# Self-attention with the scale inside the exponential and the division after the values' product

## The chip, the cores and the metric

The kernel runs on one core of one Trainium2 chip. The core has a matrix engine (TensorE, PE in the profile), a vector engine (VectorE, DVE), an activation engine (ScalarE, ACT), GpSimd (POOL) and a queue engine (SyncE, SP), each with its own in-order stream of instructions; they wait for one another by semaphores. The metric is the device time of one execution in microseconds. The time before is 3067.56 us, the median of three runs (3067.09 to 3067.82).

## The reference

Four layers act on 128 tokens of 256 features. Each layer has a cross attention over a context of 12544 tokens, a self-attention among the 128 tokens, and a feed-forward part with experts; each adds to the residual. The change touches the self-attention of layers 1, 2 and 3 (layer 0 has another kind). Cut to what matters:

```
layer 1:  a1 = softmax(q1 k1 / 4);  a2 = softmax(q2 k2 / 4)     # 16 heads, each split in two halves of 8
          out = (a1 - lam * a2) @ v;  out = out / rms(out) * norm_w * 0.2
layer 2:  out = softmax(rope(q) rope(k) / 4) @ v                # 16 heads of 16
layer 3:  out = softmax(where(causal, q k / 8, -inf)) @ v       # 16 heads of 64
```

Layer 1 has thus 32 score matrices of 128 x 128, layers 2 and 3 have 16 each.

## The kernel before, in words

A class `Net` writes the whole program as one trace of tile operations. A scheduler then puts the instructions of each engine in an order: except in stretches that the kernel holds in order by hand (`in_order`, in the cross attentions), an engine's order need not be that of the source. Tiles come from pools with a fixed number of buffers, and an instruction that needs a buffer waits until the last reader of its former content is done.

`run` (L1730) goes through the layers: cross attention, self-attention, feed-forward. While layer 1's self-attention runs, the first eight key and value blocks of layer 2's cross attention are made as well (`keys_biased`, L977, called from L1758): PE projects the context (L102) into the one PSUM pair `kv`, ACT empties it into keys (L132) and values (L136), and only then can the next block use the pair. Their context tiles `ctxA` and `ctxB` are loaded through GpSimd's queue (L393, L395). In layer 2 the weights of the experts and the few tokens `lastA`, `lastB` for layer 3 are loaded during the self-attention, through SP's queue.

The self-attention's core is a generator, `weights_among` (L1291). For each group it spreads the keys over heads with a mask (`keys`, L1298, on DVE), and then makes tiles of four score matrices, 128 queries by 4 x 128 keys, in one PSUM bank `ps` (L278 through `mm`); there are three such banks in this stage. Each tile goes through these steps:

- DVE scales the scores out of PSUM into `e` (L296 through `ts`), or in layer 3 scales and adds the causal mask in one operation (L292 through `stt`);
- `softmax` (L469): maximum (L473), subtraction (L289 through `tt`), both on DVE; exponential on ACT (L475); sum (L477), reciprocal (L478) and division, a product with the broadcast reciprocal (L289), on DVE.

`values_among` (L1315) turns the weights by PE (`tr`, L1320), copies them to SBUF as `eT` (in turn DVE L284 and ACT L286), multiplies with the values into `acc` (L278) and copies the result to `o` (L1326, DVE). Layer 1 first combines the two halves of each head, `a = e0 + lam * e1` (L1368, L292 through `stt`), so that its tile of four matrices gives two heads. There are eight tiles in layer 1, four in layer 2 and four in layer 3. Tiles `e` have three buffers, `tr` two banks, `acc` one.

After its loop layer 1 normalises `o` (L1371 to L1381, with a square root on ACT, L1377), copies it to `turned`, multiplies by `wo` (L278) and adds the residual. The normalisation of the next part makes `xn` (L298), which PE turns (`tr`, L450) for the router.

Of the kernel before, what the change touches and what calls it, by code (L numbers as in the profile page):

```python
# [16 lines left out]
AF = mybir.ActivationFunctionType  # L17
ALU = mybir.AluOpType
AX = mybir.AxisListType
PSUM = bass.MemoryType.PSUM  # L20

P = 128
# [22 lines left out]
def bc(ap, axis, n):  # L45

    ap = ap.unsqueeze(axis)
    shape = list(ap.shape)
    shape[axis] = n
    return ap.to_broadcast(shape)  # L50
# [155 lines left out]
class Net:  # L206
# [1083 lines left out]

    def weights_among(self, pool, qT, kT, ng, hpg, mask, scale, causal=None):  # L1291

        nc = self.nc
        per = max(1, 4 // hpg)
        for g in range(0, ng, per):
            keys = pool.tile([P, per, hpg, P], F32, tag="keys", name="keys")
            for i in range(per):
                self.tt(keys[:, i], bc(kT[:, g + i, :], 1, hpg), bc(mask, 2, P), ALU.mult)  # L1298
            for a in range(0, per * hpg, 4):
                p = self.ps()  # L1300
                if per > 1:
                    for i in range(per):
                        self.mm(p[:, i * hpg * P : (i + 1) * hpg * P], [(qT[:, g + i, :], keys[:, i].rearrange("p h t -> p (h t)"))])
                else:
                    self.mm(p, [(qT[:, g, :], keys[:, 0, a : a + 4, :].rearrange("p h t -> p (h t)"))])
                p = p.rearrange("p (h t) -> p h t", h=4)
                e = pool.tile([P, 4, P], F32, tag="e", name="e", bufs=3)
                if causal is None:
                    self.ts(e, p, scale, None, ALU.mult)
                else:  # L1310
                    self.stt(e, p, scale, bc(causal, 1, 4), ALU.mult, ALU.add)
                self.softmax(e, e, (4, P))
                yield g * hpg + a, e

    def values_among(self, pool, out, h, e, n, v, hd):  # L1315

        nc = self.nc
        t = self.tr()
        for i in range(n):
            nc.tensor.transpose(t[:, i, :], e[:, i, :], self.ident)  # L1320
        eT = pool.tile([P, 4, P], F32, tag="eT", name="eT")
        self.evac(eT[:, :n], t[:, :n])
        p = self.acc()
        for i in range(n):
            self.mm(p[:, i * hd : (i + 1) * hd], [(eT[:, i, :], v[:, (h + i) * hd : (h + i + 1) * hd])])
        nc.vector.tensor_copy(out[:, h * hd : (h + n) * hd], p[:, : n * hd])  # L1326

    def dot_exp(self, pool, a, b):
        d = self.d
# [8 lines left out]
    def l1_attn(self, x):  # L1338
        nc, d = self.nc, self.d
        with self.tc.tile_pool(name="a1", bufs=2, reuse_waits="tile") as pool:  # L1340
            wqkv = self.load_w(d["L1_attn_w_qkv"], 2, 3 * D, "wqkv")
            wo = self.load_w(d["L1_attn_wo"], 2, D, "wo")
            norm = self.all_rows(d["L1_attn_norm_w"], D, "norm", pool)
            m8 = self.group_mask(16, 8, 1.0, "m8g")
            l1, l2 = self.dot_exp(pool, "q1", "k1"), self.dot_exp(pool, "q2", "k2")
            lam = pool.tile([P, 1], F32, tag="lam", name="lam", bufs=1)
            self.tt(lam, l2, l1, ALU.subtract)
            self.ts(lam, lam, LAMBDA_INIT, None, ALU.subtract)

            xT = self.normed(x)  # L1350
            qT = pool.tile([P, 2, P], F32, tag="qT", name="qT", bufs=1)
            kT = pool.tile([P, 2, P], F32, tag="kT", name="kT", bufs=1)
            for i, t in ((0, qT), (2, kT)):
                for g in range(2):
                    p = self.ps()
                    c = slice((i + g) * P, (i + g + 1) * P)
                    self.mm(p[:, :P], [(wqkv[:, k, c], xT[:, k, :]) for k in range(2)])
                    self.evac(t[:, g, :], p[:, :P])
            v = pool.tile([P, D], F32, tag="v", name="v", bufs=1)
            p = self.ps()  # L1360
            self.mm(p[:, :D], [(xT[:, k, :], wqkv[:, k, 2 * D :]) for k in range(2)])
            self.evac(v, p[:, :D])

            o = pool.tile([P, D], F32, tag="o1", name="o1", bufs=1)
            for h, e in self.weights_among(pool, qT, kT, 2, 16, m8, 0.25):
                pairs = e.rearrange("p (h two) t -> p h two t", two=2)
                a = pool.tile([P, 2, P], F32, tag="a", name="a")
                self.stt(a, pairs[:, :, 1, :], lam, pairs[:, :, 0, :], ALU.mult, ALU.add)  # L1368
                self.values_among(pool, o, h // 2, a, 2, v, 16)

            heads = lambda t: t.rearrange("p (h e) -> p h e", h=H)  # L1371
            t = pool.tile([P, D], F32, tag="sq", name="sq")
            self.tt(t, o, o, ALU.mult)
            r = self.stat()
            nc.vector.tensor_reduce(r, heads(t), AX.X, ALU.add)
            self.ts(r, r, 1.0 / 16, 1e-6, ALU.mult, ALU.add)
            nc.scalar.activation(r, r, AF.Sqrt)  # L1377
            nc.vector.reciprocal(r, r)
            self.ts(r, r, 1.0 - LAMBDA_INIT, None, ALU.mult)
            self.tt(heads(o), heads(o), bc(r, 2, 16), ALU.mult)  # L1380
            self.tt(o, o, norm, ALU.mult)  # L1381

            turned = pool.tile([P, 2, 16, 8], F32, tag="turned", name="turned", bufs=1)
            for c in range(2):
                nc.vector.tensor_copy(turned[:, c], o.rearrange("p (g c e) -> p c e g", c=2, e=16)[:, c])
            p = self.ps()
            self.mm(p[:, :D], [(turned[:, c].rearrange("p e g -> p (e g)"), wo[:, c, :]) for c in range(2)])
            return self.residual(x, p[:, :D])

    def l2_attn(self, x):  # L1390
        nc, d = self.nc, self.d
        with self.tc.tile_pool(name="a2", bufs=2, reuse_waits="tile") as pool:
            w = [self.load_w(d[f"L2_attn_{k}T"], 2, D, k) for k in ("wq", "wk", "wv", "wo")]
            turns = pool.tile([P, 2, 8], F32, tag="turns", name="turns", bufs=1)
            nc.sync.dma_start(turns, d["rope"])
            cos, sin = turns[:, 0, :], turns[:, 1, :]
            xT = self.normed(x)
            qkv = pool.tile([P, 3, D], F32, tag="qkv", name="qkv", bufs=1)
            for i in range(3):
                p = self.ps()  # L1400
                self.mm(p[:, :D], [(xT[:, k, :], w[i][:, k, :]) for k in range(2)])
                self.evac(qkv[:, i, :], p[:, :D])
            qk = qkv[:, :2, :].rearrange("p i (h e two) -> p (i h) e two", e=8, two=2)
            roped = pool.tile([P, 2 * H, 8, 2], F32, tag="roped", name="roped", bufs=1)
            re, im = qk[:, :, :, 0], qk[:, :, :, 1]
            c, s = bc(cos, 1, 2 * H), bc(sin, 1, 2 * H)
            t = pool.tile([P, 2 * H, 8], F32, tag="t", name="t", bufs=1)
            self.tt(roped[:, :, :, 0], re, c, ALU.mult)
            self.tt(t, im, s, ALU.mult)
            self.tt(roped[:, :, :, 0], roped[:, :, :, 0], t, ALU.subtract)  # L1410
            self.tt(roped[:, :, :, 1], re, s, ALU.mult)
            self.tt(t, im, c, ALU.mult)
            self.tt(roped[:, :, :, 1], roped[:, :, :, 1], t, ALU.add)
            qkT = self.transposed(roped.rearrange("p h e two -> p (h e two)"), 4, pool, "qkT")
            o = self.ap.tile([P, D], F32, tag="o", name="o")
            for h, e in self.weights_among(pool, qkT[:, :2], qkT[:, 2:], 2, 8, self.m16, 0.25):
                self.values_among(pool, o, h, e, 4, qkv[:, 2, :], 16)
            return self.project_out(x, o, w[3])

    def l3_attn(self, x):  # L1420
        nc, d = self.nc, self.d
        dims = H * 64
        with self.tc.tile_pool(name="a3", bufs=2, reuse_waits="tile") as pool:
            causal = pool.tile([P, P], F32, tag="causal", name="causal", bufs=1)
            nc.gpsimd.memset(causal, 0.0)
            nc.gpsimd.affine_select(
                out=causal, in_=causal, pattern=[[-1, P]], compare_op=ALU.is_ge, fill=NEG, base=0, channel_multiplier=1
# [18 lines left out]
                self.evac(v[:, n : n + 512], p)  # L1446
            wo = self.load_w(d["L3_attn_w_o"], 8, D, "w_o")
            o = pool.tile([P, dims], F32, tag="o3", name="o3", bufs=1)
            for h, e in self.weights_among(pool, *qkT, 8, 2, self.m64, 0.125, causal):
                self.values_among(pool, o, h, e, 4, v, 64)  # L1450
            return self.project_out(x, o, wo, pool=pool, n=8)


# [368 lines left out]
```

## Time and profile before

| what | time |
|---|---|
| median of three runs | 3067.56 us |
| the profiled execution | 3067.74 us |
| its span, first to last instruction | 3066.0 us |
| PE busy | 2916.9 us (95%) |
| DVE busy | 2233.8 us (73%) |
| ACT busy | 1436.4 us (47%) |
| POOL busy | 457.6 us (15%) |
| mean granted TensorE clock | 0.969 |
| loop of layer 1's self-attention | 1211.5 to 1251.9 us of the span |
| loop of layer 2's | 1848.3 to 1872.95 us |
| loop of layer 3's | 2955.3 to 2982.5 us |

The span is that of one execution under the hardware profiler, 1.74 us shorter than the device time of that execution. Busy times are sums over the whole span; a matmul of 32-bit floats shows as two records. The granted clock is what the chip let TensorE run at in a stretch, as a share of full speed. In the rows below, `out<-in` names the tile an instruction writes and those that it reads, and "idle before, releaser" says how long its engine had stood and what it then waited for. Line numbers are those of the kernel before.

### The profile page before, as it was taken

To read this page: it belongs to the slowest core of one execution; us is meant where nothing else is said; L and a number is where in the kernel's file an instruction comes from. 1 tells how busy PE (TensorE), PEld (TensorE's weight loads), DVE (VectorE), ACT (ScalarE), POOL (GpSimd) and SP (SyncE) were. 2 spreads that over 40 slices of the span, in tenths; PEclk is the share of its full clock that TensorE was granted. 3 is DMA by queue.
4 is the path that set the end of the run, shared out by engine and by line. 5 is a ranking of instruction groups with operands and counts; after the bars stand their busy time and mean duration, and the time that the engine had idled before them with its cause. 6 is when DMAs were issued, how large, how long until landed. Compare 5 with 4: busy or idle time off the path is not lost.

```text
span 3066.0 us, 78435 instructions
## 1 busy us (share of the span) xinstructions
PE 2916.9 (95%) x34893; PEld 2205.6 (72%) x34893; DVE 2233.8 (73%) x2864; ACT 1436.4 (47%) x1694; POOL 457.6 (15%) x502
## 2 busy tenths in 40 slices
PE   8999999989999998899999997999999999999979
PEld 5677667455676576765776664689989889889858
DVE  6876877549997897779668754367777777777844
ACT  1176148321582285211852571355556556556521
POOL 6676676212000000110000000100000000000000
PEclk9999999999999999899999996999999999999979
DMA  4201210561002202421012015432222222222436
GB/s 128 61 19 32 68 40 4 192 218 56 21 3 73 63 5 91 150 78 42 18 37 70 24 30 180 145 97 85 86 78 87 84 81 86 80 85 84 122 112 208
DMA packets 166857, 246.95 MB, mean 81 GB/s; under 512 B 21261, under 2 KB 108431, under 8 KB 166520
## 3 DMA queue, kind: packets, MB, share of 16 engines
q1 hardware_dynamic: 160200, 227.67, 24.2%
q0 software_dynamic: 6208, 14.27, 1.6%
q8 instruction: 274, 4.49, 0.6%
q14 instruction: 63, 0.52, 0.1%
q10 hardware_dynamic: 112, 0.01, 0.0%
HBM read 241.75 MB, written 0.13 MB: 79 GB/s over the span
## 4 chain that ended last, share of the span: by engine, by line
PE 81%; DVE 11%; issue 3%; ACT 2%; POOL 2%; DMA 2%; SPq 0%; DVEq 0%; POOLq 0%; ACTq 0%
PE pair L102 19%; PE pair L551 9%; PE v L102 8%; PE acc L658 8%; PE sc L796 6%; PE acc L838 6%; PE pair L592 4%; PE ps L278 4%; PE one L592 4%; DVE parts L552 4%; PE kv L102 2%; DVE e L292 2%; PE acc L278 2%; PE pair L585 2%; PE ps L1609 1%
## 5 line engine op out<-in xcount | busy, mean ns | idle before, releaser
L552 DVE TENSOR_REDUCE parts<-pair 128x2 f32<-128x1024 f32 x600 | 679.1, 1197 | 103.6 <-PE pair L551 101.8
L102 PE MATMUL pair<-ctxA,wk 128*128 128x256 f32 x1236 | 329.0, 399 | 1.4 <-ACT kT L193 1.1
L102 PEld LDWEIGHTS pair<-ctxA,wk 128*128 128x128 f32 x1236 | 217.2, 190 | 140.6 <-DVE parts L552 95.2
L551 PE MATMUL pair<-kT,qz 32*128 32x512 f32 (+1 forms) x1632 | 270.1, 608 | 6.9 <-DVE parts L552 6.8
L289 DVE TENSOR_TENSOR top<-top,kept 128x1024 f32<-128x1024 f32 (+2 forms) x145 | 169.1, 1169 | 134.4 <-ACT kept L798 133.2
L798 ACT COPY kept<-sc 128x1024 f32<-128x1024 f32 (+1 forms) x135 | 136.3, 1010 | 252.0 <-PE sc L796 252.0
L292 DVE SCALAR_TENSOR_TENSOR e<-pair,floor 128x1024 f32<-128x1024 f32 x196 | 230.4, 1219 | 9.1 <-PE pair L592 3.0
L612 ACT ACTIVATE e<-e 128x1024 f32<-128x1024 f32 x196 | 207.2, 1057 | 45.5 <-DVE e L292 38.1
L636 ACT ACTIVATE e<-pair 128x1024 f32<-128x1024 f32 x196 | 200.6, 1024 | 53.0 <-PE pair L592 32.2
L592 PE MATMUL pair<-qz,kT 32*128 32x256 f32 x2112 | 219.1, 374 | 0.0
L658 PE MATMUL acc<-e,v 128*17 128x128 f32 x6336 | 211.4, 274 | 3.1 <-ACT e L651 2.2
L536 POOL TENSOR_SCALAR row<-mask 128x512 bf16<-128x512 uint8 (+1 forms) x100 | 189.8, 1898 | 151.3 <-PE pair L551 96.7
L132 ACT ACTIVATE kT<-pair,bk 128x512 f32<-128x512 f32 (+1 forms) x68 | 45.9, 675 | 350.1 <-PE pair L102 350.1
L292 DVE SCALAR_TENSOR_TENSOR e<-one,maskcol,less 128x256 f32<-128x256 f32 x392 | 162.6, 477 | 60.4 <-PE one L592 43.3
L651 ACT ACTIVATE e<-e 128x1024 f32<-128x1024 f32 x196 | 205.0, 1048 | 0.0
L658 PEld LDWEIGHTS acc<-e,v 128*17 128x17 f32 x6336 | 155.9, 97 | 67.9 <-ACT e L651 44.9
L796 PE MATMUL sc<-qz,kT 64*128 64x128 f32 x2816 | 197.8, 279 | 0.0
L102 PEld LDWEIGHTS v<-wv,ctxA 128*128 128x128 f32 x1568 | 190.9, 193 | 6.6 <-issue 2.0
L102 PE MATMUL v<-wv,ctxA 128*128 128x128 f32 x1568 | 194.2, 277 | 0.0
L289 DVE TENSOR_TENSOR e<-one,less 128x512 f32<-128x512 f32 x196 | 126.2, 686 | 89.0 <-PE pair L592 84.4
L102 PE MATMUL pair<-ctxB,wk 64*128 64x256 f32 x1236 | 188.9, 399 | 0.0
L796 PEld LDWEIGHTS sc<-qz,kT 64*128 64x128 f32 x2816 | 171.6, 187 | 13.0 <-issue 1.3
(450 smaller groups left out, 5477.4 us busy)
## 6 DMA issues: line engine op xcount, KB each, us to landing
ctxA<-in_ctxA SPq DMA_DIRECT2D x324, 256.0 KB
ctxB<-in_ctxB SPq DMA_DIRECT2D x339, 128.0 KB
w<-in_L_ffn_W SPq DMA_DIRECT2D x32, 1024.0 KB
ctxA<-in_ctxA POOLq DMA_DIRECT2D x36, 256.0 KB, 3.0
w<-in_L_ffn_w_gateT SPq DMA_DIRECT2D x8, 1024.0 KB
wu<-in_L_ffn_w_upT SPq DMA_DIRECT2D x8, 1024.0 KB
w<-in_L_ffn_w_downT SPq DMA_DIRECT2D x8, 1024.0 KB
w<-in_L_ffn_w1T SPq DMA_DIRECT2D x8, 1024.0 KB
```

The lines of the kernel that those rows point to most:

```text
L102: self.nc.tensor.matmul(out, a, b, start=start and not low, stop=low == 1, skip_group_check=True)
L289: self.nc.vector.tensor_tensor(out, a, b, op)
L292: self.nc.vector.scalar_tensor_tensor(out, a, s, b, op0, op1, **kw)
L536: nc.gpsimd.tensor_scalar(row[:, :n], to[:, :n], 0.0, 1.0, ALU.is_gt, ALU.subtract)
L551: nc.tensor.matmul(x[:, i, :n], qz[r, g, s, :], keys.kT(b)[r, :n], start=not masked, stop=True)
L552: nc.vector.tensor_reduce(parts[:, s, 2 * half : 2 * half + 2, b], x[:, :, :n], AX.X, ALU.max)
L592: nc.tensor.matmul(at, keys.kT(c // 4)[tiles[t], k], q, start=start, stop=True, skip_group_check=True)
L612: nc.scalar.activation(to, to, AF.Exp)
L636: nc.scalar.activation(to, pair, AF.Exp)
L651: nc.scalar.activation(to, to, AF.Exp)
L658: nc.tensor.matmul(acc[32 * t : 32 * t + 17, half, :], v[:, c % 4 + j, 4 * half + t, :], es[half][:, t // 2, j, t % 2, :], start=c + j + h ...
L796: nc.tensor.matmul(x[:, t, c : c + P], kT[r, c : c + P], qz[r, g, :], start=True, stop=True)
```

## The change

The softmax is written out in `weights_among`. Where there is no causal mask, the maximum and the subtraction read the scores straight out of PSUM, unscaled, and the scale is an argument of the exponential. With the causal mask, scaling and mask stay one operation as before. The weights are not divided any more: the generator yields the reciprocals of the sums, and `values_among` multiplies the values' product by them as it takes it out of PSUM, in place of the copy. Layer 1, whose halves have different sums, combines them with the ratio of the two reciprocals times `lam`, one operation for each of the two heads, and divides by the first sum at the end. The function `softmax` remains for its other users.

```diff
     def weights_among(self, pool, qT, kT, ng, hpg, mask, scale, causal=None):
...
                 e = pool.tile([P, 4, P], F32, tag="e", name="e", bufs=3)
-                if causal is None:
-                    self.ts(e, p, scale, None, ALU.mult)
-                else:
+                if causal is not None:
                     self.stt(e, p, scale, bc(causal, 1, 4), ALU.mult, ALU.add)
-                self.softmax(e, e, (4, P))
-                yield g * hpg + a, e
-
-    def values_among(self, pool, out, h, e, n, v, hd):
+                    p = e
+                m = self.stat(4)
+                nc.vector.tensor_reduce(m, p, AX.X, ALU.max)
+                self.tt(e, p, bc(m, 2, P), ALU.subtract)
+                nc.scalar.activation(e, e, AF.Exp, scale=scale if causal is None else 1.0)
+                s = self.stat(4, "sum4")
+                nc.vector.tensor_reduce(s, e, AX.X, ALU.add)
+                nc.vector.reciprocal(s, s)
+                yield g * hpg + a, e, s
+
+    def values_among(self, pool, out, h, e, r, n, v, hd):
...
-        nc.vector.tensor_copy(out[:, h * hd : (h + n) * hd], p[:, : n * hd])
+        heads = lambda t: t.rearrange("p (h e) -> p h e", h=n)
+        self.tt(heads(out[:, h * hd : (h + n) * hd]), heads(p[:, : n * hd]), bc(r, 2, hd), ALU.mult)
...
-            for h, e in self.weights_among(pool, qT, kT, 2, 16, m8, 0.25):
+            for h, e, r in self.weights_among(pool, qT, kT, 2, 16, m8, 0.25):
+
+                two = r.rearrange("p (h two) -> p two h", two=2)
+                ratio, first = self.stat(2, "ratio"), self.stat(2, "first")
+                nc.vector.tensor_copy(first, two[:, 0])
+                nc.vector.reciprocal(ratio, two[:, 0])
+                self.stt(ratio, ratio, lam, two[:, 1], ALU.mult, ALU.mult)
                 pairs = e.rearrange("p (h two) t -> p h two t", two=2)
                 a = pool.tile([P, 2, P], F32, tag="a", name="a")
-                self.stt(a, pairs[:, :, 1, :], lam, pairs[:, :, 0, :], ALU.mult, ALU.add)
-                self.values_among(pool, o, h // 2, a, 2, v, 16)
+                for i in range(2):
+                    self.stt(a[:, i], pairs[:, i, 1], ratio[:, i : i + 1], pairs[:, i, 0], ALU.mult, ALU.add)
+                self.values_among(pool, o, h // 2, a, first, 2, v, 16)
```

Layers 2 and 3 pass the reciprocals on to `values_among` in the same way. The scheduler orders the instructions anew: those of PE, DVE and ACT change places within the three stages. Two of the eight key blocks that PE makes beside layer 1's self-attention are now emptied after it, and of SP's loads one context pair in layer 1 and two pairs of expert weights in layer 2 are issued later in the order.

More of the change, by code (lines that the diff above doesn't have):

```diff
@@ L1415, in l2_attn @@
             o = self.ap.tile([P, D], F32, tag="o", name="o")
-            for h, e in self.weights_among(pool, qkT[:, :2], qkT[:, 2:], 2, 8, self.m16, 0.25):
-                self.values_among(pool, o, h, e, 4, qkv[:, 2, :], 16)
+            for h, e, r in self.weights_among(pool, qkT[:, :2], qkT[:, 2:], 2, 8, self.m16, 0.25):
+                self.values_among(pool, o, h, e, r, 4, qkv[:, 2, :], 16)
             return self.project_out(x, o, w[3])
@@ L1448, in l3_attn @@
             o = pool.tile([P, dims], F32, tag="o3", name="o3", bufs=1)
-            for h, e in self.weights_among(pool, *qkT, 8, 2, self.m64, 0.125, causal):
-                self.values_among(pool, o, h, e, 4, v, 64)
+            for h, e, r in self.weights_among(pool, *qkT, 8, 2, self.m64, 0.125, causal):
+                self.values_among(pool, o, h, e, r, 4, v, 64)
             return self.project_out(x, o, wo, pool=pool, n=8)
```

## The prediction

> **What bounds the kernel now.** I read the page first: over the whole span TensorE (PE) is busy 95%, VectorE (DVE) 73%. That is an average over stages of different kinds, and the change touches only the loop of `weights_among` and `values_among`, so I looked for where that loop runs and asked for busy times by stretch. Columns: stretch, length, busy time of PE, of its weight loads, of DVE, ScalarE (ACT) and GpSimd, the granted TensorE clock, DMA share, GB/s.
>
> ```profile
> 1211.50:1252.00 40.50, 33.80 (x197) 24.34 (x195) 31.69 (x70) 13.57 (x25) 3.22 (x6) 0.96 0.27 82
> 1252.00:1260.60 8.60, 2.79 (x7) 1.49 (x7) 4.86 (x16) 2.48 (x4) 0.57 (x2) 0.53 0.11 34
> 1260.60:1267.50 6.90, 6.90 (x38) 6.90 (x39) 2.28 (x8) 1.49 (x2) 0.23 (x1) 0.60 0.15 42
> 1846.00:1873.00 27.00, 17.25 (x58) 12.00 (x58) 16.38 (x32) 5.18 (x8) 0.00 (x0) 0.63 0.71 248
> 2955.00:2982.50 27.50, 17.61 (x68) 13.72 (x68) 17.84 (x35) 4.88 (x8) 0.44 (x2) 0.58 0.14 48
> ```
>
> The loops of layers 1, 2 and 3 (first, fourth, fifth row) take 95 of 3066 us. In none is an engine full: tiles hand work from engine to engine. The second and third rows are the tail of layer 1's attention and the start of its feed-forward part. Next the waits inside layer 1's loop (who <- whom: us, times, longest):
>
> ```profile
> ACT kv L132 <- PE kv L102: 13.0, 5, 3.6
> DVE o L1326 <- PE acc L278: 4.9, 6, 1.7
> PE kv L102 <- ACT kv L136: 4.8, 5, 1.3
> DVE eT L284 <- PE tr L1320: 1.9, 3, 1.3
> DVE st L477 <- ACT e L475: 1.8, 3, 0.8
> ```
>
> In layer 1 PE also makes the key blocks of the next cross attention (L102), one PSUM pair at a time; each waits until ACT has emptied the last. DVE stands 8.8 us (40.5 - 31.7), PE 6.7 us. Both matter, so a gain on DVE alone is not a gain of the loop. Layers 2 and 3 have no such filler, and there the chain of the work that ended last shows one tile after another (start, us, what; layer 2):
>
> ```profile
> 1863.15 0.22 DVE o L1326
> 1863.37 0.61 DVE e L289
> ...
> 1864.03 1.13 PE tr L1320 x4
> ...
> 1865.18 0.70 DVE eT L284
> ...
> 1865.93 1.91 PE acc L278 x8
> ...
> 1867.86 0.22 DVE o L1326
> ```
>
> The division (`e` L289) sits straight in it, ahead of the transposes: the last ones each wait for it.
>
> **What the change removes and adds.** DVE's rows in layer 1's loop (count | busy us, mean ns):
>
> ```profile
> L289 DVE TENSOR_TENSOR e<-e,st 128x512 f32<-128x512 f32 x16 | 10.5, 682 | 0.0
> L473 DVE TENSOR_REDUCE st<-e 128x4 f32<-128x512 f32 x8 | 5.4, 673 | 0.0
> L296 DVE TENSOR_SCALAR e<-ps 128x512 f32<-128x512 f32 x8 | 5.3, 678 | 0.0
> L292 DVE SCALAR_TENSOR_TENSOR a<-e,lam 128x256 f32<-128x256 f32 x8 | 3.8, 480 | 0.1
> L1326 DVE COPY o<-acc 128x32 f32<-128x32 f32 x8 | 1.5, 192 | 4.9 <-PE acc L278 4.9
> L478 DVE RECIPROCAL st<-st 128x4 f32<-128x4 f32 x8 | 1.3, 168 | 0.0
> ```
>
> Layer 1, a tile: out go the scaling 0.68, the division 0.68 and the combination 0.48; in come a copy and a reciprocal of 128x2 (0.15 and 0.17, as the 128x1 and 128x2 reciprocals of this trace), a ratio (0.17), and two 128x128 combinations (0.34 each, the row `ahead` of that shape). Net -0.67 us, times 8: DVE 31.7 to 26.4. The product that replaces the copy out of `acc` keeps its price: 128x128 `o<-pair,st`, PSUM times a broadcast reciprocal, takes 0.287 against 0.281 for a copy. Layer 2, a tile: -1.36, times 4. Layer 3, a tile: only the division, -0.68, times 4, since scaling and mask stay in one operation. The exponential with a scale costs what it did: L1545, a sigmoid with a scale on 128x512, takes 630 ns; the exponentials take 629.
>
> [...] The trace has the very operation: a reduction of 128x512 out of PSUM (L552) takes 679 ns, out of SBUF 673 to 680; scaling from PSUM takes 678. By the rows it costs 0, and I take that.
>
> **Layer 2, walked through the issue order of the changed kernel.** The score products end as before (first at 1848.3, then 1850.0, 1850.9, 1851.7). DVE: maximum 0 to 1849.0, subtraction 0 to 1849.75, maxima and subtractions 1 and 2 to 1852.7 with 0.6 per operation back to back. Exponentials end 1850.4, 1852.75, 1853.4. Transposes of tile 0 no longer wait for sum and division: 1851.5, not 1854.66. `acc` of tile 0 runs from 1854.3 behind half of tile 2's transposes. From there the order is worse than it need be: the fourth tile's subtraction stands behind the product out of tile 2's `acc`, so tile 3 runs alone: subtract 0.68, exp 0.64, tr 1.13, eT 0.59, acc 1.91, product 0.22. With every `acc` at the 1.9 us of the half clock the last product ends at 1867.15, with the first two at full clock (tr took 0.66 in 1854.7) at 1865.15, against 1872.95: -5.8 to -7.8. I take -6.5.
>
> **Layer 3, likewise.** The order puts the first two tiles' transposes, then both `acc` (1.97 each), ahead of the last score product; tile 2's maximum and subtraction stand behind the products out of `acc` 0 and 1 (2964.95, 2966.9), tile 3's subtraction behind that of `acc` 2 (2972.9). The last transposes start 2974.6, not 2978.22: -3.6 us; the rest is as before. Bounds -2 (two more half-microsecond waits in that order) and -4.6 (PE at full clock for one `acc`).
>
> **Layer 1's loop.** Six key blocks were emptied in it; now four are, and a fifth is nearly through; the rest follows behind. One block less on PE is 2.9 us (27 us of L102 rows, overlapping, in six blocks) and its wait about 1.0 (4.8/5): by PE -3.9. By DVE -5.3. Walking the order as above gives the last product near 1243.5, or -8, since both reliefs act in turn. I take -6, between. Bounds 0 (the stalls grow as DVE shrinks) and -8.
>
> **Layer 1's tail.** The sixth block now runs here, and is a new wait: its first key product stands ahead of the output product L278 (wo) in PE's queue and waits for ACT, which empties the fifth block (0.69 + 0.58) only after the square root L1377. DVE meanwhile needs 1.75 us from the root to `turned`; the wait ends 2.05 us after the root: +0.3. Its other products, 2.4 us, stand ahead of the transposes of `xn`, which come 2.25 us after wo: +0.2. ACT empties it ahead of the exponential's table load (1.27 + 1.28), ready when `probs` is. Without that cover the block would cost its full 4.2 us. Against this stands the clock. PE is idle in 68% of the tail, and the feed-forward start then runs at 0.60. [...] I take -1, tail -0.5 in sum; bounds +1.5 and -2.5.
>
> **What lies behind.** Every gain is carried to the end only if nothing else is late. After 1876 layer 2's chain is PE products to 1976, with no DMA in it; layer 3's from 2991.45 to 3062.6 likewise; layer 1's runs over DVE, GpSimd and ACT. SP's queue: in layer 2 two of eight 1 MB weight loads (and then those of the next expert, which wait for PE) move behind the bias and `lastA` loads, which wait for the end of the attention; at 350 GB/s they land some 6 us later, around 1880, and their expert starts after 1920: 0. The next expert's hold up `qd`, `od`, `ou` and the router, needed only in layer 3: 0. In layer 1 one context pair moves behind the bias and `wq`, needed a stage later; GpSimd's queue waits on the same key blocks as before, for data two blocks ahead: 0.
>
> **Sum.** -6.5 (layer 1: -6 and -0.5) - 6.5 - 3.6 = -16.6 us. The profiled execution took 3067.74 (span 3066.0 and 1.74 around it), so 3051.1; the median is 0.2 lower: 3051.0. Its own range is 3047 to 3056.
>
> **Rivals.** (1) PE's queue keeps layer 1: the loop is held by the key blocks, those moved pay in the tail, layer 1 gains 1; layers 2 and 3 at their low ends -4 and -2: 3060.5. For it: L102 and ACT's emptying fill most of layer 1's chain. Against: PE had 6.7 us of gaps. 19%. (2) More: layer 1 -8 and -2.5 by the clock, -7.8, -4.6: 3044.7. 11%. (3) Slower, by PSUM banks: of three `ps` banks each is now freed after the subtraction, not after the first read. In layer 1 five score products need a freed bank, and behind each stand key blocks, transposes and `acc` on PE, whose products stand before the next subtraction on DVE. If each held PE for a tile's serial chain, about 5.65 us, that is +28 against -15.4 of the rest (5.3, 6.5, 3.6): near 3080. It decides from 3.1 us each. Against: such a product never waited in the trace of before, and in the new order the subtractions run two tiles ahead of the products out of `acc`. 4%. (4) The change works, and something later gives it back (a weight load, the router): 3067. No DMA is in the chains named. 4%. The forecast has 62%.
>
> About 0.2% (6.1 us) is what a measurement of this kernel can tell from no change. Faster by more, under 3061.4: 62 + 11 + 17 of (1) = 90%; within: 2 + 4 = 6%; slower: 4%. The range 3044 to 3061 leaves out some 8 of (1), 4 of (2), and the 8 of (3) and (4).
>
> **What would show it.** Layer 1's last product out of `acc` 6 us after the keys earlier than now (34 us, not 40), with DVE near 26 us busy; layer 2's from first maximum to last product 17 to 19 us, not 24.6; layer 3's last transposes 19.3 us after its first tile, not 22.9; reductions and subtractions out of PSUM at 0.68. Wrong would be: PE waiting in front of score products for a subtraction, wo more than 4 us behind the last product of layer 1, or 0.75 us for PSUM reads.

## The result and the profile after

The changed kernel takes 3046.86 us (median of six runs, 3040.41 to 3052.98) against 3067.69 us for the kernel before in the same comparison: a ratio of 0.9932, 95% interval 0.9919 to 0.9945, so 16.9 to 24.8 us faster. Two later comparisons of the same pair gave 0.9931 [0.9916, 0.9946] and 0.9939 [0.9925, 0.9953]. The forecast of 3051.0 had the sign; the time lies in its wide range (3044 to 3061) and 0.1 us under its narrow one (3047 to 3056). One of its four terms came out quite differently in the first profile, though, and the experiments are mostly about that one.

First the stretches again, of the changed kernel's first profiled execution (3045.77 us, span 3044.0): layer 1's loop, the normalisation behind it up to `turned`, from there by `wo` to the first `pre` of the feed-forward part, then the loops of layers 2 and 3. Columns as in the prediction: stretch, length, busy PE, weight loads, DVE, ACT, POOL, granted clock, DMA share, GB/s.

```profile
1206.72:1246.35 39.63, 36.95 (x167) 26.16 (x168) 24.79 (x84) 11.98 (x21) 3.22 (x6) 0.78 0.22 68
1246.35:1249.58 3.23, 1.60 (x12) 1.30 (x9) 2.74 (x9) 1.27 (x3) 0.30 (x2) 0.81 0.33 103
1249.58:1257.98 8.40, 7.59 (x52) 6.50 (x51) 2.52 (x9) 3.89 (x6) 0.28 (x1) 0.87 0.34 101
1834.66:1857.77 23.11, 15.93 (x62) 10.61 (x62) 12.44 (x24) 6.81 (x9) 0.00 (x0) 0.66 0.65 244
2937.50:2960.09 22.59, 15.45 (x67) 12.20 (x65) 15.26 (x31) 4.69 (x7) 0.44 (x2) 0.66 0.15 52
```

Between the same marks before took 40.31, 3.23, 10.09, 30.51 and 26.94 us. Its three loops:

```profile
1211.62:1251.93 40.31, 33.68 (x197) 24.22 (x195) 31.50 (x69) 13.50 (x25) 3.22 (x6) 0.96 0.27 81
1843.00:1873.51 30.51, 18.81 (x62) 12.90 (x62) 17.44 (x33) 6.84 (x9) 0.00 (x0) 0.61 0.73 256
2955.31:2982.26 26.95, 17.06 (x67) 13.23 (x65) 17.60 (x35) 4.59 (x7) 0.44 (x2) 0.57 0.13 45
```

Layers 2 and 3 gained 7.4 and 4.35 us. Layer 1's loop gained 0.7 us only, although DVE has 6.7 us less to do in it (24.8 for 31.5) and four key blocks are emptied in it instead of six (PE has x167 matmuls, before x197). The clock column says where to look: 0.78, where before had 0.96. Three stretches whose code is the same before and after were 4.9 us (start to layer 1's keys), 1.1 and 2.1 us (between the layers) shorter here; that is taken up below.

Next the waits inside layer 1's loop (who <- whom: us, times, longest):

```profile
ACT eT L286 <- PE tr L1326: 16.8, 4, 7.3
DVE o L289 <- PE acc L278: 13.4, 8, 5.1
...
ACT kv L132 <- PE kv L102: 8.1, 4, 2.4
...
PE ps L278 <- DVE e L289: 0.2, 1, 0.2
```

DVE's wait for `acc` grew from 4.9 to 13.4 us: with the work taken off DVE, this loop now ends on PE, and PE's granted clock is 0.50 in its second half (1227.86 to 1244.92). `ACT kv L132` shows 4 emptied blocks, as forecast. The last line is rival (3): one score product waits 0.2 us for a bank that the subtraction holds, where that rival needed 3.1 us from each of five, so it is out.

The operations have the lengths that the prediction gave them (layer 1's loop, by shape; count | busy us, mean ns | idle before, releaser):

```profile
L1317 DVE TENSOR_REDUCE st<-e 128x4 f32<-128x512 f32 x8 | 5.3, 678 | 0.0
L1313 DVE TENSOR_REDUCE st<-ps 128x4 f32<-128x512 f32 x8 | 5.3, 678 | 0.9 <-PE ps L278 0.9
L289 DVE TENSOR_TENSOR e<-ps,st 128x512 f32<-128x512 f32 x8 | 5.3, 670 | 0.0
L292 DVE SCALAR_TENSOR_TENSOR a<-e,st 128x128 f32<-128x128 f32 x16 | 4.9, 342 | 0.0
L292 DVE SCALAR_TENSOR_TENSOR st<-st,lam,st 128x2 f32<-128x2 f32 x8 | 1.7, 212 | 0.1
L289 DVE TENSOR_TENSOR o<-acc,st 128x32 f32<-128x32 f32 x8 | 1.5, 192 | 13.4 <-PE acc L278 13.4
```

The first two rows are the same reduction, from SBUF and from PSUM: 678 ns each. The last row is the product that divides: 192 ns, as the copy it replaced.

Layer 2's chain of waits from the third `acc` to the last product (start, us, what):

```profile
1849.71 1.88 PE acc L278 x8
...
1851.61 0.23 DVE o L289
1851.83 0.61 DVE e L289
...
1852.52 0.64 ACT e L1315
...
1853.20 1.13 PE tr L1326 x4
...
1854.41 0.59 ACT eT L286
...
1855.05 1.91 PE acc L278 x8
...
1856.98 0.23 DVE o L289
```

This is the order that the prediction walked through: the division is gone from in front of the transposes, and the fourth tile's subtraction (1851.83) stands behind the product out of the third `acc`, so that tile runs alone for 5.4 us. From the first maximum (1839.53) to the last product layer 2 takes 17.7 us, as forecast (17 to 19; before 24.6).

### The profile page after: what moved, and what is told of

Same layout as the page of the kernel before. It is cut to its first block, busy times and chain, and to the rows that moved or that the text cites. A ratio compares the mean times of both kernels' runs of the same rounds, so it can differ in the third digit from the quotient of the medians.

```text
span 3044.0 us, 78454 instructions
## 1 busy us (share of the span) xinstructions
PE 2912.6 (96%) x34893; PEld 2204.4 (72%) x34893; DVE 2220.7 (73%) x2868; ACT 1436.9 (47%) x1694; POOL 458.0 (15%) x502
## 4 chain that ended last, share of the span: by engine, by line
PE 82%; DVE 11%; issue 2%; ACT 2%; DMA 1%; POOL 1%; SPq 0%; DVEq 0%; ACTq 0%; POOLq 0%
PE pair L102 20%; PE pair L551 9%; PE v L102 8%; PE acc L658 8%; PE acc L838 6%; PE sc L796 6%; PE ps L278 5%; PE pair L592 4%; PE one L592 4%; DVE parts L552 4%; PE kv L102 3%; PE acc L278 2%; DVE e L292 2%; PE pair L585 2%; PE ps L1623 1%
## 5 line engine op out<-in xcount | busy, mean ns | idle before, releaser
L102 PE MATMUL pair<-ctxA,wk 128*128 128x256 f32 x1236 | 328.9, 399 | 1.4 <-ACT kT L193 1.1
L102 PEld LDWEIGHTS pair<-ctxA,wk 128*128 128x128 f32 x1236 | 217.0, 190 | 140.5 <-DVE parts L552 95.2
L132 ACT ACTIVATE kT<-pair,bk 128x512 f32<-128x512 f32 (+1 forms) x68 | 45.9, 675 | 351.1 <-PE pair L102 351.1
L102 PEld LDWEIGHTS v<-wv,ctxA 128*128 128x128 f32 x1568 | 190.2, 192 | 6.6 <-issue 1.7
L102 PE MATMUL v<-wv,ctxA 128*128 128x128 f32 x1568 | 193.5, 276 | 0.0
L102 PE MATMUL pair<-ctxB,wk 64*128 64x256 f32 x1236 | 188.9, 399 | 0.0
```

The source lines that it names most:

```text
L102: self.nc.tensor.matmul(out, a, b, start=start and not low, stop=low == 1, skip_group_check=True)
```

## The theories and the experiments

Theory A: the change shortens layer 1's loop as forecast, and TensorE's clock took it back in that profile, by halving for 17.1 us of the loop (3.4 before). Theory B, the prediction's rival (1): the key blocks in PE's queue hold the loop, whatever DVE does. For the scaling alone there was also the question whether PSUM reads are dearer. All runs below are compared with the kernel before on the same chip.

**Parts of the change.** Layer 1 alone: layers 2 and 3 keep the former generator and `values_among` under other names. Layers 2 and 3 alone: the reverse.

```diff
-            for h, e, r in self.weights_among(pool, qkT[:, :2], qkT[:, 2:], 2, 8, self.m16, 0.25):
-                self.values_among(pool, o, h, e, r, 4, qkv[:, 2, :], 16)
+            for h, e in self.old_weights(pool, qkT[:, :2], qkT[:, 2:], 2, 8, self.m16, 0.25):
+                self.old_values(pool, o, h, e, 4, qkv[:, 2, :], 16)
```

> The change in layer 1 alone, layers 2 and 3 as before. Theory A (clock): layer 1's loop is some 8 us shorter (32 to 33 us instead of 40.4) in executions where TensorE stays at full clock in it, and about as long as before where the clock falls to half in its middle, as it did in the profiled execution (half from 1227.6 to 1244.7 us); the median time is then 5 to 9 us below before, and the times of single executions lie several us apart. Rival B (queue): the key blocks on TensorE hold the loop whatever the clock does, so the loop is 39 to 40 us in every profile and the time is at most 2 us below before, from the tail.

Measured: 3060.85 us against 3065.53, ratio 0.9986 [0.9978, 0.9995], so 1.5 to 6.7 us faster. The median lies between what A and B gave it (5 to 9, and at most 2) and decides nothing. Its profiled loop of layer 1 does speak: it took 35.06 us, with 6.8 us of it at half clock, where B had 39 to 40 in every profile.

> The change in layers 2 and 3 alone, layer 1 as before. Both theories: the loops of layers 2 and 3 are shorter by 6.9 and 5.6 us as in the profile of the changed kernel (first reading of the scores to the last product), 12.5 us together. A: the median is 11 to 14 us below before and single times lie within 4 us, as with the kernel before, since layer 1's loop is where the spread comes from. B: 18 to 20 us below before, nearly all that the whole change gave.

Measured: 3053.74, ratio 0.9960 [0.9946, 0.9974], 8.0 to 16.6 us faster, by the medians 11.8 as A had it (11 to 14) and not B (18 to 20); layer 2's stretch took 23.06 and layer 3's 22.66, as in the whole change. Layer 1's loop, here the one of before, took 43.27 us, with 10.2 us at half clock, against 40.31 with 3.4. A's other sign missed: single runs were to lie within 4 us here, since the spread was to come from the changed loop of layer 1. They lie over 8.1 us (6 runs), those of the kernel before over 13.3 (39 runs) and those with layer 1 alone over 15.5 (21 runs), so layer 1's loop is not where all of the spread comes from.

The scaling alone, against the changed kernel: the weights are divided as before.

```diff
                 nc.vector.reciprocal(s, s)
-                yield g * hpg + a, e, s
+                self.tt(e, e, bc(s, 2, P), ALU.mult)
+                yield g * hpg + a, e
```

> Only the scale moves into the exponential (layers 1 and 2, maximum and subtraction read PSUM); the weights are still divided. Theory A: one vector operation of 0.68 us less in each of 12 tiles; layer 1's vector engine has 5.4 us less to do, layer 2's 2.7; median 4 to 8 us below before. Rival C (reading the scores twice out of PSUM is dearer than one copy): reductions and subtractions out of PSUM take 0.75 us and the time is within 2 us of before.

Measured: 3062.46, ratio 0.9985 [0.9977, 0.9993], 2.1 to 7.1 us faster. Layer 2's stretch went from 30.51 to 26.84, layer 3's stayed at 26.94 (it has no such scaling), layer 1's loop took 40.53 with 9.2 us at half clock, and the normalisation behind it 2.3 us longer, which was not followed up. The total is 3.1 us by the medians, between A's 4 to 8 and rival C's 2; but its reductions out of PSUM took 676 ns, not the 750 that C asked for.

The division alone, against the changed kernel: the scores are scaled into `e` first.

```diff
                 if causal is not None:
                     self.stt(e, p, scale, bc(causal, 1, 4), ALU.mult, ALU.add)
-                    p = e
+                else:
+                    self.ts(e, p, scale, None, ALU.mult)
+                p = e
...
-                nc.scalar.activation(e, e, AF.Exp, scale=scale if causal is None else 1.0)
+                nc.scalar.activation(e, e, AF.Exp)
```

> Only the division moves behind the values' product; the scores are still scaled into SBUF first. Theory A: layers 2 and 3 lose the division from the path to the transposes, 0.7 us and its wait in each of 8 tiles: 6 to 9 us below before in these; layer 1 gains nothing on the vector engine (0.68 and 0.48 go, 1.17 come). Median 6 to 10 below before. Rival B: the same in layers 2 and 3, and layer 1 a little longer.

Measured: 3045.33, ratio 0.9939 [0.9925, 0.9952]: the division alone is worth as much as the whole change, twice what was expected of it. Layer 2 took 24.41, layer 3 22.69, layer 1's loop 36.13 with 3.4 us at half clock and five key blocks emptied in it.

**The same kernel again, and two edits of layers 2 and 3.** If A holds, the same program must show other lengths of layer 1's loop when the clock falls differently.

> The changed kernel itself once more, for its spread and for a second profile of layer 1's loop. Theory A (the clock took layer 1's gain): the loop, from the last keys to the square, takes 31.4 us plus half of the time that TensorE runs at half clock in it; with less than 7 us of that it is under 35 us. Theory B (the key blocks hold it): near 39.6 us again, whatever the clock. The median: 3047, within 2 us of the division alone (3045.3) by A; the two differ by more than 4 us if the scaling within the exponential costs something.

Measured: 3045.84, ratio 0.9931 [0.9916, 0.9946]. Its loop of layer 1:

```profile
1205.88:1240.98 35.10, 32.27 (x168) 22.96 (x168) 24.73 (x86) 11.97 (x21) 3.22 (x6) 0.90 0.26 79
```

Same instructions, same DVE time (24.7), 4.5 us shorter, with 6.8 us at half clock and not 17.1. Its wait of DVE for `acc` is shorter as well:

```profile
DVE o L289 <- PE acc L278: 9.5, 8, 4.2
```

B asked for 39.6 whatever the clock; it falls. In eight of the profiled executions, those below among them, layer 1 is the changed kernel's. Its loop comes in two kinds only (lengths in us; half clock summed from the trace's clock records):

| layer 1's loop | length | of it at half clock |
|---|---|---|
| as before: profile before; layers 2 and 3 alone | 40.31; 43.27 | 3.4; 10.2 |
| as changed, short: changed kernel (2nd), layer 1 alone, earlier subtractions (1st), filled PE | 34.88 to 35.09 | 6.8 |
| as changed, long: changed kernel (1st and 3rd), earlier subtractions (2nd), both edits | 39.43 to 39.64 | 17.1 |
| division alone, two profiles | 36.13; 36.33 | 3.4 |
| scaling alone | 40.53 | 9.2 |

Within the changed code (39.5 - 35.0) / (17.1 - 6.8) = 0.44 us are lost for each us at half clock; within the code of before (43.27 - 40.31) / (10.2 - 3.4) = 0.44 too. Taken down to no half clock by that slope, the loop is 38.8 us before and 32.0 changed. So by this estimate, which goes beyond what any profile showed, the change is worth 6.8 us there at equal clock, the key block that left the loop included.

What sets the kind is not how busy PE is ahead of the fork. The stretches of one clock step just before and after the fork, first in the first profile, then in the second:

```profile
1224.35:1227.76 3.41, 2.97 (x20) 2.02 (x18) 2.65 (x9) 1.67 (x4) 1.07 (x2) 1.00 0.27 77
1227.76:1231.18 3.42, 3.20 (x11) 2.84 (x12) 2.37 (x10) 0.76 (x2) 0.00 (x0) 0.51 0.16 43
```

```profile
1223.26:1226.67 3.41, 2.94 (x19) 2.03 (x18) 2.65 (x9) 1.67 (x4) 1.07 (x2) 1.00 0.27 77
1226.67:1230.10 3.43, 3.24 (x19) 2.61 (x19) 3.22 (x14) 0.73 (x2) 0.00 (x0) 1.00 0.14 43
```

Both stretches before the fork have the same work (PE busy 2.97 and 2.94 of 3.41 us), and then the clock falls in one and stays in the other. In these eight profiles the instructions of DVE and ACT in the loop stand in one order. The one difference found is a matter of phase: the clock changed in steps of 3.4 us here (it stayed at half for 6.83, 17.07 and 3.41 us around this loop in the first profile), and the last half-clock stretch ahead of the loop ended 2.8 to 3.1 us before the loop's start in the four long loops and 3.3 to 3.7 us before it in the four short ones. No run set the phase, so that it is the cause is not shown.

Now the two edits. In the first, all four tiles' subtractions stand ahead of the products out of `acc`:

```diff
+            tiles = list(self.weights_among(pool, *qkT, 8, 2, self.m64, 0.125, causal, bufs=4))
+            for h, e, r in tiles:
+                self.values_among(pool, o, h, e, r, 4, v, 64, after=self.sub)
...
         self.tt(heads(out[:, h * hd : (h + n) * hd]), heads(p[:, : n * hd]), bc(r, 2, hd), ALU.mult)
+        if after is not None:
+            self.tc.add_manual_dep(nc.cur_bb.bb.instructions[-1], after.name, info, reason="in order")
```

> In layers 2 and 3 all four tiles' subtractions stand ahead of the first product out of acc (four buffers of e). If the order on DVE is what still holds these loops, as the timelines of the changed kernel say, the last tile no longer runs alone: layer 2 22.9 down to 19 to 20.5 us, layer 3 22.6 down to 19 to 20.5, in sum 4 to 7 us faster than the changed kernel, near 3041. If PE at half clock holds them (1.9 us for each acc, one bank), it is 1 us or less in each. Layer 1 is the changed kernel's: its loop is again 31.4 plus half of its half-clock time by A, 39.6 by B.

Measured: 3043.47, ratio 0.9927 [0.9913, 0.9940]. Layer 3's stretch fell from 22.59 to 16.69 us (and from its first tile to the first `pre` behind `wo` from 34.7 to 27.7), layer 2's only from 23.2 to 22.05; 19 to 20.5 was expected of each. In layer 3 the clock is a part of it (3.4 us at half clock for 15.3). The last two `acc` of layer 3 in the timeline of the changed kernel's first profile (start, us, what, idle before and releaser), and then of the edit's second run:

```profile
2952.24 1.97 PE L278 MATMUL acc<-v,eT 128*128 128x64 f32 x8 [0.78 <-DVE eT L284]
...
2957.90 1.97 PE L278 MATMUL acc<-v,eT 128*128 128x64 f32 x8
```

```profile
2948.51 1.10 PE L278 MATMUL acc<-v,eT 128*128 128x64 f32 x8
...
2950.23 1.07 PE L278 MATMUL acc<-v,eT 128*128 128x64 f32 x8 [0.38 <-DVE o L289]
```

They are 5.66 us apart in the one, since the last tile runs alone, and 1.72 us in the other, at nearly twice the speed. In layer 2, 14.3 us stayed at half clock (15.4 without the edit), and the earlier order gave 1.2 us.

The second edit fills PE with transposes of the identity, which the real ones overwrite:

```diff
         t = self.tr()
+        if n == 4:
+            for i in range(4):
+                nc.tensor.transpose(t[:, i, :], self.ident, self.ident)
...
         p = self.acc()
+        if n == 4:
+            for i in range(2):
+                nc.tensor.transpose(p[:, :P], self.ident, self.ident)
```

> In layers 2 and 3 each tile has four idle transposes of the identity ahead of its own and two ahead of its values' product, written over at once. If it is the gaps on PE that let its clock fall in these loops, half-clock time falls from 15 us to under 7 in each, and with it 2 to 4 us of each loop: near 3042. If the clock doesn't answer to so little work, the fillers only cost their own time, 0 to +2 us in each loop: 3047 to 3051. Layer 1 is the changed kernel's: 31.4 plus half by A, 39.6 by B.

Measured: 3044.14, ratio 0.9927 [0.9912, 0.9942]. Layer 2's stretch took 21.83 with 10.6 us at half clock. In layer 3 all four `acc` ran in 1.00 to 1.19 us. Its stretch ends early (16.93, with 3.4 us at half clock) because the scheduler now put the first product with `wo` ahead of the last `acc`. From its first tile to the first `pre`, which that does not touch, it took 30.8 us for 34.7, with 9.3 us at half clock for 20.5. By the rows of its last two tiles (1.97 + 1.97 - 1.10 - 1.00) + (1.06 + 1.12 - 2 x 0.66) = 2.7 us of the 3.9 are the faster clock (`acc`, transposes). The schedule also put the third tile's subtraction 0.6 us earlier on DVE, so the idle work is not the only difference, and no run separates the two.

The phases that occurred don't explain the half clock of layer 3. In the six profiles with its instructions in the changed kernel's order (three of the changed kernel, layers 2 and 3 alone, and the division alone twice) the clock came back from its first fall 7.1 to 7.9 us after the first tile, and each time 14.8 to 15.5 us of the stretch were at half clock. In the four with an edit it came back after 7.8 to 7.9 us, and 3.4 were.

> Both edits of layers 2 and 3. If order and clock each hold the loops, the gains add up: 6 to 11 us under the changed kernel, 3036 to 3041, and it is the fastest of all. If the earlier order already closes the gaps on PE, the fillers add nothing to it: the same as the order alone, within 2 us. Layer 1 is the changed kernel's: 31.4 plus half by A, 39.6 by B.

Measured: 3043.86, ratio 0.9926 [0.9911, 0.9940]; layer 3 took 28.6 us to its first `pre` (27.7 by the order alone), layer 2 23.94 with 16.3 us at half clock. As in the second of the two expectations, the two do not add up, and layer 2 is 0.8 us longer with both than with neither; why is open.

**Once more, beside each other.**

> The changed kernel beside the two below, to set its median on more runs: 3046, within 2 us of the two times before. Its layer 1 loop is again one of two kinds, near 35 us with 6.8 us of half clock or near 39.6 with 17.1: theory A holds 31.9 us plus 0.45 of the half-clock time for either.

Measured: 3045.08, ratio 0.9939 [0.9925, 0.9953]; the loop is of the long kind, 39.50.

> The division alone once more. Taken by the stages, the scaling within the exponential adds some 2.7 us in layer 1's loop at full clock and 1.3 in layer 2's, so the division alone should stand 4 us above the changed kernel, near 3050. If it stands within 1.5 us of it again, the scaling adds nothing to the division in the total, whatever it does to its stage.

Measured: 3045.23, ratio 0.9937 [0.9925, 0.9949]. The 4 us did not show: on top of the division the scaling adds nothing to the total. The stages suggest why. It takes 1.2 us from layer 2 (23.1 for 24.3). In layer 1 it would take 2.7 us at equal clock (36.2 - 0.44 x 3.4 = 34.7, against 32.0; PE also has 107 matmuls of key blocks in that loop for 114, so not all of it need be the scaling's). But with it the loop spends 6.8 or 17.1 us at half clock, half of the eight profiles each, and without it 3.4 in both: 0.44 x (12 - 3.4) = 3.8 us come back. For the division alone that rests on two profiles, one in either phase (3.0 and 3.4 us).

> The earlier subtractions once more, to tell whether the 7 us by which layers 2 and 3 were shorter reach the end. If the rest is chance of the clock, its median is 4 to 8 us under the changed kernel of this call, and layer 3's loop again takes near 16.7 us with 3.4 at half clock. If TensorE falls to half clock elsewhere in its place, the medians stay within 2 us and the stages after the two loops are longer again.

Measured: 3041.39, ratio 0.9927 [0.9912, 0.9941]; layer 3 took 16.70 again with 3.4 us at half clock, layer 2 21.90. It has the lowest medians, 2.4 and 3.7 us under the changed kernel beside it, but the intervals overlap. Over 11 runs its mean is 3042.4 against 3045.7 over the changed kernel's 12 beside them, with standard deviations of 4.4 and 5.2 us of single runs. Its layers 2 and 3 are some 8 us shorter; whether the clock takes the rest back elsewhere or the median is only too rough for it, these runs do not say.

## Why the prediction was right, and where not

**Sizes of the operations: right.** All durations taken from rows of before held. Only the ratio was longer (212 ns for 170). DVE's work in layer 1's loop fell further than forecast (24.8, not 26.4), because small operations overlap: rows of 150 to 210 ns were added at their length, and on DVE some start 70 to 80 ns after each other (1213.71, 1213.78 and 1213.86 in the first profile, with 0.16 us for each of the first two).

**PSUM reads: the row was right.** In layer 1's loop the same reduction takes 678 ns from either memory and the subtraction out of PSUM 670, and the scaling alone was a gain (2.1 to 7.1 us), not a loss. No row shows the 0.75 us that the prediction and rival C name for a read of PSUM; in layer 2 the reduction and the subtraction out of PSUM take 688 and 682 ns.

**Layer 2, -6.5: right, -7.4.** The walk through the issue order had the tile that runs alone, and as its end it gave -5.8 to -7.8, by how many `acc` run at full clock. Two did (0.96 and 1.07 us), the last two at 1.86 and 1.89.

**Layer 3, -3.6: right in mechanism, too small by 0.75.** The walk took 1.97 us for each `acc`; the first two took 1.10 and 1.08. The bound of -4.6 had allowed one of them. The last transposes started 18.55 us after the first tile (forecast 19.3, before 22.9). 0.4 us came back behind `wo`.

**Layer 1's tail, -0.5: too small, -1.7.** From `turned` to `pre` it went from 10.09 to 8.40. The new wait for the key block cost 0.7 (forecast 0.3): from `turned` to the residual 2.69 us, before 1.98. The transposes of `xn` did not wait at all (0.2). The rest, -2.4, I put down to the clock: 2.2 us at half clock in this stretch against 10.1. No run shows the -1 that the forecast takes for the clock, nor the -2.5 of its bound; both were my choice. From the row of before one can work out at most 2.8 for it, also an estimate: 6.90 us at a clock of 0.60 are 4.1 at full clock. The -2.4 is nearer to that.

**Layer 1's loop, -6: right at equal clock, wrong as a time.** At equal clock it is -6.8. In the three profiles of the changed kernel it was -0.7, -5.2 and -0.8. The step that failed is "By PE -3.9. By DVE -5.3. ... I take -6": it holds the clock of the loop at the 0.96 of before, and the clock was counted in the tail only. The missing term is 0.44 us for each us more at half clock than before, 1.5 us of loss in the short kind and 6.0 in the long. PE is not the idler for it: it stood for 6.6 us of this loop before and for 2.7 and 2.8 in the first two profiles of the changed kernel. One part of the sum has no row behind it, too: a key block was put at 2.9 us of PE, where the rows of L102 cover 22.15 us of the loop before in six blocks, 3.7 each, and "By PE" would be -4.7. Over the eight profiles the loop is 37.3 on average, against 41.8 over the two with layer 1 as before: -4.5.

**The sum.** With these averages: -4.5 (loop) - 1.7 (tail) - 7.4 (layer 2) - 4.35 + 0.4 (layer 3) = -17.5, against -16.6 forecast and -20.8 measured [-24.8, -16.9]. That forecast and sum are so close is in part luck: the loop fell short of its term by 1.5 us, the other three went beyond theirs by 2.5. The first profile is 22 us shorter by its span, and 8.1 us of that lie in the three stretches of equal code named above. The stretch ahead of layer 1's keys took 1203.1 to 1216.0 us in the thirteen profiles, the shortest with 34.1 us at half clock and the longest with 58.0, though only the kernels' later code differs. So I count that part to the clock's chance and not to the change; the interval of the medians does not need it. It is an argument, not shown: the three longest of the thirteen (1210.9 to 1216.0) belong to the three kernels that still divide the weights of layers 2 and 3, and the medians of all three comparisons, 20.8, 19.3 and 20.3 us, lie 2 to 3 us above the sum by stages. Where those come from is open.

**Rivals.** (1) falls with the second profile of the changed kernel, whose loop is 5.2 us shorter with the same key blocks. (2), more by 7.8 in layer 2 and 4.6 in layer 3, was near for those two, not for layer 1 as it ran. In total the time lies nearer to (2), 3044.7, than to the forecast. (3) and (4) did not occur: one score product waited 0.2 us for a bank, and the part behind layer 3's `pre` took 71.8 us (before 72.0).

## What to carry to other kernels

When work is taken off another engine, the matrix engine's clock can take back what was won, even where the matrix engine has less idle time than before (here 6.0 of 6.8 us in layer 1's loop, with PE standing for 2.7 us and not 6.6): write a term for the clock into the sum of the stage that is changed, not only into what follows it, and read the granted clock of that stage in more than one profile before a gain or loss is explained. A division that commutes with a matrix product belongs behind it, where the operand is small and an operation reads it anyway (here 192 ns on 128x32, as the copy it replaced, for 0.68 us on 128x512). In a chain of few tiles, ask which tile's first step stands behind another tile's last one in an engine's queue.

## What the runs showed of the hardware

In these profiles TensorE's clock fell to 0.50 for stretches of 3.4 us and multiples of it (3.4, 6.8, 10.2 and 17.1 in the first profile of the changed kernel), also right after a stretch in which PE was busy 87% of the time (2.97 of 3.41 us). Two profiles of one program, with the same work up to the fork, differed by 10.3 us of half clock and 4.5 us of time in a 35 us loop, and the phase of those steps against the work separated the two kinds in eight of eight. That the phase causes the fork was not tried. PE stood for 0.44 of the 3.41 us before the fall (3.41 - 2.97). PE's busy share of a stretch alone does not tell whether the clock falls after it: in the profile before, it stayed up behind 1.70 of 3.42 us busy (641.49 to 644.91) and fell behind 3.41 of 3.41 (1969.28 to 1972.69).

In layer 3, an earlier order of DVE's subtractions brought the time at half clock, from the first tile to the first `pre`, from 20.5 to 6.2 us, and a few idle transposes on PE (with one subtraction earlier) to 9.3. The second took the time of that part from 34.7 to 30.8 us, for an edit that does more work on PE. In layer 2 the same transposes took 1.4 us (23.2 to 21.8), and with the earlier order nothing.
